# Norm statistics spread by transfers, the image kept in DRAM, two frames, three z tiles and a compact recurrence in a two-layer convolution and attention kernel

## The chip, the cores and the metric

The kernel runs on one core of one Trainium2 chip. The metric is the device time of the whole program in microseconds (us); before the change the median of three runs is 5973.05 us (5971.22 to 5975.53).

## The reference

The input is 32 images of 128 channels and 64 x 64 pixels, all in float32. Layer 0 adds to each image a 3 x 3 convolution of its group-normalized self, with a kernel mixed for each image from four. Layer 1 treats an image as 4096 tokens of 128 channels. It normalizes each token over the channels (norm 1), adds a gated windowed attention (windows of 144, step 72, 4 heads of 4, on 16 channels), normalizes the sum again (norm 2) and adds that to the layer's input; this sum is called x2 here. Then x2 is normalized (norm 3), multiplied by a matrix, batch-normalized over all tokens of all images, and run through a recurrence over the 4096 tokens; its states are added to x2.

```
x = x + conv(gn(x), dyn_k)                       # layer 0
t = to_tokens(x)                                 # 32 x 4096 tokens of 128
n = ln_t(t)                                      # norm 1
out = n + sigmoid(gate) * up(attention(down(n)))
t = t + (out - mean(out)) / sqrt(var(out) + 1e-5) * ln_gamma + ln_beta   # norm 2; this t is x2
Wx = einsum('bti,hi->bth', ln_t(t), W)           # norm 3
Wx = (Wx - mean) * rsqrt(var + 1e-5) * gamma + beta      # over all tokens
step: yt = sigmoid(wx_t + yt @ V.T)
x = from_tokens(t + ys)
```

## The kernel before

Channels lie on the 128 partitions and tokens along the free dimension. Two stages follow each other.

The first stage, `images` (line 331), goes over the 32 images. For each image there are seven jobs, written as Python generators: `load` (fetch, group statistics, mixing of the kernel), `conv`, `project` (norm 1, down projection, queries, keys, values), `attend` (28 steps: scores into the four-bank PSUM tile `sc`, an exponential on ACT, a weighted sum with the exponential as the moving operand), `divide` twice (softmax denominators, up projection into the image's `zt`), and `tail` (norm 2, x2 and its store to the output, norm 3, the product by W, the store of z to DRAM for the second stage). The jobs yield before each step and name the engine, the PSUM tile and the operands that the step needs. A planner in the program that builds the kernel (class `Clock`, line 41, and the loop at line 1074) keeps for each engine the time at which it would be free and takes, among the open jobs, the step that could start first; its prices are in `cost` (line 116). For SP, the engine that issues transfers, it counts 0.8 us of SP for each transfer and a landing time that depends on its size and on the length of its rows. It has no shared DMA bandwidth. The priority of the jobs is the image's number plus an offset for each job (line 1073); `conv` comes last and fills. So the order on each engine is written out when the program is built and doesn't change when something is late: each engine runs its own list in order, and SP does too.

A frame `xs` is a padded image of 66 x 66; there are three, and image b stays in its frame from the fetch until `tail` has added it to make x2. A `zt` tile (4096 tokens) holds an image from norm 1 to the store of z; there are two. The frames' rows are 64 elements, so a fetch moves 256 B pieces; zt is stored in rows of 8 KB.

Norm 1 subtracts the mean by a product with a centring matrix `cen` (8 products of 512 columns, evicted by DVE into zt; `centre`, line 580). `deviations` (line 526) works on half an image: ACT squares, PE sums over the channels with the matrix `avg`, whose result holds different tokens on a few partitions, and `inv_dev` makes the inverse square root from a logarithm, an exponential and four DVE steps. `spread` (line 564) brings these rows back to all 128 partitions by 8 products with `row` into the `sc` tile; DVE multiplies zt by it. This happens for norm 1, norm 2 and norm 3, twice an image each. All operations of this stage are recorded by the planner's helper, so the profile gives line 168 for all of them; they are told apart by their tiles.

The second stage, `by_runs` (line 1541), cuts the 4096 tokens of an image into 128 runs of 32 and starts each run 20 steps early, so that 128 runs advance side by side. A group is two images, 256 columns. Four streams take four groups each; a step is a product with V (PE, into a PSUM tile), a scaled addition of z (DVE, into `h`) and a sigmoid (ACT). In the 20 warming steps the state is in `yw`, which is compact; in the 32 real steps the state is written into the z tile at `zt[:, :, :, r]`, where neighbouring columns lie 32 elements apart, and the next product reads it there (lines 1584 to 1593). Stream j starts 13 j rounds after the first (line 1605). At a group's end GpSimd issues two accumulating transfers that add its states to the output, and SP loads the group six further on into the z tile that comes free (six tiles).

Of the kernel before, what the change touches and what calls it, by code (L numbers as in the profile page):

```python
# [13 lines left out]
P = 128  # L14
EPS = 1e-5
H = W = 64
T = H * W
# [23 lines left out]
class Clock:  # L41
# [22 lines left out]
    @staticmethod  # L64
    def span(ap):

        dims = [(int(s), int(n)) for s, n in ap.ap]
        lo = int(ap.offset) % max(dims[0][0], 1)
        return lo, lo + sum(s * (n - 1) for s, n in dims[1:]) + 1
# [8 lines left out]
    def spot(self, ap):  # L78

        t = ap.tensor  # L80
        if type(t).__name__ != "Tile":
            return None
# [9 lines left out]
    def after(self, eng, ap, write):  # L92
        at = 0.0
        p = self.spot(ap)
        if p is None:
            return at
        lo, hi = self.span(ap)
        psum = "PSUM" in p[0][1].upper()
        for l, h, end, e, w in self.seen.get(p, ()):
            if e != eng and (write or w or psum) and (psum or (l < hi and lo < h)):  # L100
                at = max(at, end + self.LAG)
        return at
# [81 lines left out]
def hybrid_kernel(  # L184
# [34 lines left out]
    k_d = dram.tile([NK, P, 4, 3, P], F32, name="k_d")  # L219
    z_d = dram.tile([NB, P, T], F32, name="z_d")  # L220
# [109 lines left out]

    def images(nc):
# [6 lines left out]
        with ExitStack() as pa:  # L338

            frm = pa.enter_context(tc.tile_pool(name="frm", bufs=1))  # L340
            xs = [frm.tile([P, H + 2, W + 2], F32, name=f"xs{i}") for i in range(3)]
# [4 lines left out]
            def fetch(b):  # L346
                for i in range(4):
                    nc.sync.dma_start(rows(xs[b % 3], 16 * i, 16), x[b, :, 16 * i : 16 * i + 16, :])

            for b in range(3):  # L350
                fetch(b)
# [17 lines left out]
            big = pa.enter_context(tc.tile_pool(name="big", bufs=2))  # L369
# [93 lines left out]
            for q in range(4):  # L463
# [20 lines left out]
            row = kept([P, 2, P], "row")  # L484
            r4 = kept([P, 2], "r4")
            nc.vector.tensor_reduce(
                r4,
                ident.rearrange("p (q r) -> p r q", q=4)[:, 0:2],
                axis=AX.X,
                op=ALU.add,  # L490
            )
            nc.vector.tensor_copy(
                row, r4.rearrange("p (r o) -> p r o", o=1).to_broadcast([P, 2, P])
            )

# [30 lines left out]
            def deviations(src, h, name, mean=False):  # L526

                parts = src[:, part(h)].rearrange("p (c r t) -> p r c t", r=2, t=UNIT)
                for r in range(2):
                    yield "ACT", None, (src[:, part(h)],)  # L530
                    sq = two.tile([P, 4, UNIT], F32, name="sq")
                    nc.scalar.activation(sq, parts[:, r], AF.Square)
# [3 lines left out]
                    if mean and r == 0:  # L536
                        for i in range(2):
                            for c in range(4):
# [5 lines left out]
                                    stop=(i == 1),  # L544
                                )
                    for c in range(4):
# [5 lines left out]
                            stop=(r == 1),  # L552
                        )
                rs = two.tile([P, UNIT], F32, name=name)
                var = ps[:, 0:UNIT]
                if mean:
                    nc.scalar.activation(rs, ps[:, UNIT : 2 * UNIT], AF.Square)
                    nc.vector.tensor_max(sq[:, 1], var, rs)
                    var = sq[:, 1]
                    nc.vector.tensor_sub(var, var, rs)  # L560
                inv_dev(rs, var, sq[:, 0])
                return rs

            def spread(rs):
                ps = sc_tile()
                for r in range(2):
                    for c in range(4):
                        nc.tensor.matmul(
                            ps[:, c, UNIT * r : UNIT * (r + 1)],
                            row[32 * c : 32 * c + 32, r],  # L570
                            rs[32 * c : 32 * c + 32],
                            start=True,
                            stop=True,
                        )
                return ps.rearrange("p c t -> p (c t)")
# [4 lines left out]
            def centre(src, dst, h):  # L580

                for i in range(4 * h, 4 * h + 4):
                    s = slice(i * BLK, (i + 1) * BLK)
                    xi = rows(src, 8 * i)
                    yield "PE", "nm", (xi,)
                    ps = nm_tile()
                    nc.tensor.matmul(ps, cen, xi, start=True, stop=True)
                    nc.vector.tensor_copy(dst[:, s], ps)

            def load(b):  # L590

                while (
                    (b and ("load", b - 1) not in done)
                    or (b > 1 and ("conv", b - 2) not in done)
                    or (b > 2 and ("x2", b - 3) not in done)
                ):
                    yield
                gx = xs[b % 3]
                ks4 = []

                def kernel(k):
                    ks4.append(two.tile([P, 12, P], F32, name="kx"))
                    nc.sync.dma_start(ks4[k], k_d[k].rearrange("p j i l -> p (j i) l"))

                if b > 2:
# [47 lines left out]
                yield "DVE", None, (co, ks4[0])  # L653
                wb = two.tile([P, 12, P], F32, name="wb")
                nc.vector.tensor_scalar_mul(wb, ks4[0], co[:, 0:1])
                for k in range(1, NK):
                    if k + 1 < NK:
                        yield "SP", "kx", ()
                        kernel(k + 1)
                    yield "DVE", None, (co, ks4[k])  # L660
                    nc.vector.scalar_tensor_tensor(
                        wb, ks4[k], co[:, k : k + 1], wb, ALU.mult, ALU.add
                    )
                done["load", b] = wb, gm2

            def conv(b):
# [10 lines left out]
                gx = xs[b % 3]  # L677
# [43 lines left out]
            def project(b):  # L721

                while (
                    ("conv", b) not in done
                    or (b and ("proj", b - 1) not in done)
                    or (b > 1 and ("tail", b - 2) not in done)
                ):
                    yield
                xt = done["conv", b]
                zt = big.tile([P, T + 8], F32, name="zt")  # L730
                nc.gpsimd.memset(zt[:, T:], 0.0)
                rs = []
                for h in range(2):
                    yield from centre(xt, zt, h)
                    rs.append((yield from deviations(zt, h, "rs")))
                for h in range(2):
                    yield "PE", "sc", (rs[h],)
                    ps = spread(rs[h])
                    nc.vector.tensor_mul(zt[:, part(h)], zt[:, part(h)], ps)
# [23 lines left out]
                while b and ("sets", b - 1) not in done:  # L763
                    yield
# [7 lines left out]
                gf = gt.rearrange("p c m d -> p (c m d)")[:, 0:GT]  # L772
                yield "PE", "sc", (gt,)
# [3 lines left out]
                for i, wt in enumerate((wqB, wkB)):  # L777
                    for c in range(2):
# [17 lines left out]
                gtt = xb.rearrange("p u t -> p (u t)")[:, 0 : NWG * P].rearrange("p (m g k) -> p m g k", m=NWG, g=8)  # L796
                nc.gpsimd.tensor_copy(
                    gtt,
                    gf.rearrange("p (m r d) -> p m r d", r=9, d=DK)[:, :, 8:9].to_broadcast(
                        [P, NWG, 8, DK]  # L800
                    ),
                )
# [34 lines left out]

            def attend(b):

                while ("proj", b) not in done or (b and ("div", b - 1, 1) not in done):  # L840
# [883 lines left out]
```

## Time and profile before

| What | Value |
|---|---|
| median of three runs | 5973.05 us |
| the profiled execution | 5971.81 us |
| its span, first to last instruction | 5969.7 us |
| mean granted TensorE clock | 0.945 |
| last step of the images' stage (statistics of z) | 5251.0 us |
| first load of z for the recurrence | 5255.5 us |
| last accumulating store issued | 5944.7 us |

The page gives for each engine its busy time, the span in 40 slices, the transfers, and the costliest groups of instructions with their count, total and mean duration. A slice is 149 us, so the first 35 are the images and the rest the recurrence. HBM traffic is 237.46 MB read and 204.47 MB written. PE's busy time is modelled at the ends of matmuls, so a PE that is busy needn't be at its peak. An fp32 product of N columns appears as two instructions.

### The profile page before, as it was taken

The numbers are of one execution on the slowest core, as the hardware profiler recorded it, in microseconds if no ns is written. First come the engines' busy times: TensorE is split into PE (matmuls) and PEld (weight loads), VectorE is DVE, ScalarE is ACT, GpSimd is POOL, SyncE is SP. The second block draws the span as 40 slices with busy tenths as digits, with TensorE's granted clock in tenths as the row PEclk, the third lists the DMA queues.
The fourth block names the chain that finished last, engine by engine and source line by source line (L and its number), as shares of the span: only waits on it lengthen the run. The fifth ranks groups of instructions, "written<-read, shape, count | busy, mean of one in ns | idle before, by whom it ended". The sixth has DMA issues, their size and how long they took to land. (4 is left out here: it accounts for less than half of the span.)

```text
span 5969.7 us, 107020 instructions
## 1 busy us (share of the span) xinstructions
PE 5209.3 (87%) x46003; PEld 2542.0 (43%) x46003; DVE 3654.7 (61%) x5181; ACT 2558.7 (43%) x3756; POOL 1270.2 (21%) x1049
## 2 busy tenths in 40 slices
PE   2989999999999999999999999899989997669996
PEld 1444444444444444444444444444444443325552
DVE  4555666666666666666666656666566654348884
ACT  0343344433434434444444444344333343348884
POOL 1221222222222222222222222222222221000000
PEclk9999999999999999999999999999999998769996
DMA  5022122221112222222222222122221120046886
GB/s 123 23 66 66 55 66 60 59 66 53 59 55 60 65 66 66 66 66 66 66 66 66 66 66 66 57 64 59 59 58 55 53 60 31 31 198 177 232 204 120
DMA packets 338005, 457.22 MB, mean 77 GB/s; under 512 B 282976, under 2 KB 291440, under 8 KB 308848
## 3 DMA queue, kind: packets, MB, share of 16 engines
q1 hardware_dynamic: 328816, 383.12, 20.5%
q0 software_dynamic: 8704, 67.11, 5.6%
q8 instruction: 368, 6.03, 0.4%
q14 instruction: 117, 0.96, 0.1%
HBM read 237.46 MB, written 204.47 MB: 74 GB/s over the span
## 5 line engine op out<-in xcount | busy, mean ns | idle before, releaser
L168 ACT ACTIVATE ex<-sc 128x1152 f32<-128x1152 f32 x896 | 1013.2, 1131 | 1711.8 <-PE sc L168 1702.3
L168 PE MATMUL nm<-ut,wb 128*128 128x512 f32 x3072 | 1542.5, 630 | 12.3 <-DVE wb L168 12.3
L168 PE MATMUL sc<-qe,ks 32*128 32x288 f32 x7168 | 738.8, 483 | 333.1 <-ACT ext L168 104.6
L168 POOL TENSOR_TENSOR qe<-qs,mqk 128x576 f32<-128x576 f32 x448 | 603.5, 1353 | 1733.2 <-PE sc L168 1729.4
L168 DVE TENSOR_TENSOR xs<-xs,nm 128x512 f32<-128x512 f32 (+1 forms) x640 | 498.0, 795 | 562.8 <-PE nm L168 556.0
L168 PEld LDWEIGHTS nm<-ut,wb 128*128 128x128 f32 x3072 | 543.6, 194 | 683.0 <-issue 659.9
L168 POOL TENSOR_TENSOR ut<-xs 128x576 f32<-128x576 f32 x384 | 524.7, 1397 | 1218.3 <-issue 662.4
L168 PEld LDWEIGHTS sc<-qe,ks 32*128 32x128 f32 x7168 | 303.4, 195 | 862.2 <-issue 289.2
L168 PE MATMUL av<-ex,VE 128*32 128x144 f32 x14336 | 666.1, 307 | 3.9 <-DVE av L168 3.0
L168 ACT ACTIVATE sq<-zt 128x1024 f32<-128x1024 f32 x384 | 402.0, 1056 | 395.4 <-DVE zt L168 392.8
L168 PEld LDWEIGHTS av<-ex,VE 128*32 128x32 f32 x14336 | 377.4, 114 | 348.5 <-issue 277.6
L1587 PE MATMUL v<-zr,fVT 128*128 128x256 f32 x992 | 479.8, 622 | 39.3 <-ACT zr L1592 39.3
L168 DVE TENSOR_TENSOR zt<-zt,sc 128x2048 f32<-128x2048 f32 (+4 forms) x352 | 453.8, 1297 | 49.2 <-PE sc L168 35.1
L1592 ACT ACTIVATE zr<-h,shf 128x256 f32<-128x256 f32 x512 | 372.2, 732 | 129.9 <-DVE h L1588 84.5
L1588 DVE SCALAR_TENSOR_TENSOR h<-zr,scl,v 128x256 f32<-128x256 f32 x512 | 332.0, 651 | 137.4 <-PE v L1587 132.2
L168 PE MATMUL nm<-xs,cen 128*128 128x512 f32 x512 | 270.1, 639 | 48.4 <-DVE zt L168 48.2
L1587 PEld LDWEIGHTS v<-zr,fVT 128*128 128x128 f32 x992 | 176.5, 204 | 238.9 <-ACT zr L1592 206.5
L168 DVE TENSOR_TENSOR sq<-rs 128x256 f32<-128x256 f32 x192 | 81.6, 425 | 302.4 <-ACT rs L168 302.4
L168 DVE SCALAR_TENSOR_TENSOR zt<-sc,gbc,zt 128x576 f32<-128x576 f32 (+1 forms) x192 | 176.0, 917 | 133.4 <-PE sc L168 131.8
L168 PE MATMUL sc<-rs,row 32*128 32x256 f32 x3072 | 221.7, 403 | 34.7 <-ACT ext L168 27.5
L168 PE MATMUL nm<-zt,fWc 128*128 128x512 f32 x512 | 248.3, 617 | 1.4 <-DVE sq L168 1.3
L168 PE MATMUL nm<-sq,avg 128*32 128x256 f32 x3072 | 240.8, 394 | 8.9 <-ACT sq L168 8.9
(191 smaller groups left out, 5697.5 us busy)
## 6 DMA issues: line engine op xcount, KB each, us to landing
kx<-k_d SPq DMA_DIRECT2D x128, 768.0 KB
xs<-in_x_dram SPq DMA_DIRECT2D x128, 512.0 KB
out_dram<-zt SPq DMA_DIRECT2D x64, 1024.0 KB
z_d<-zt SPq DMA_DIRECT2D x64, 1024.0 KB
zr<-z_d SPq DMA_DIRECT2D x32, 2048.0 KB
out_dram<-zr POOLq DMA_DIRECT2D x32, 2048.0 KB, 18.3
k_d<-g SPq DMA_DIRECT2D x4, 768.0 KB
g<-in_conv_k_dram SPq DMA_DIRECT2D x4, 576.0 KB
```

The lines of the kernel that those rows point to most:

```text
L168: got = f(*args, **kw)
L1587: nc.tensor.matmul(ps, fVT, prev, start=True, stop=True)
L1588: nc.vector.scalar_tensor_tensor(h, zt[:, :, :, r], scl, ps, ALU.mult, ALU.add)
L1592: nc.scalar.activation(prev, h, AF.Sigmoid, bias=shf)
```

## The change

- Two scratch tensors in DRAM are new: `r_d` (inverse deviations, and for norm 1 also the mean times the inverse deviation) and `x_d` (the image after the convolution). The planner now tracks `r_d` as one region.
- `deviations` works on a whole image with four blocks of 1024 columns. Its results are stored to `r_d` by four small transfers. `spread` no longer uses PE: it loads quarters of 1024 tokens from `r_d` to all 128 partitions by a broadcasting transfer, into one of five tiles `place`, at most three ahead, and DVE applies them from there. The matrices `row` and the `spread` products are gone.
- Norm 1's mean is summed by PE beside the squares, and subtracted by DVE from a transfer like the deviations; `centre` and its 8 products are gone.
- The image is stored to `x_d` after the convolution, from the frame, in four transfers, and read back by quarters for x2. So a frame is free after norm 1: two frames in place of three, and three zt tiles in place of two.
- An attention may start when the first division of the one before is done, and waits for the second at its tenth set. `av` and `ext` are single tiles. The planner's offsets change.
- The mixed kernel is loaded in halves (8 transfers of 384 KB in place of 4 of 768 KB).
- In the recurrence the state alternates between two compact tiles, GpSimd copies it into the z tile, DVE writes its sum over the product in PSUM, and a stream starts 8 rounds after the one before.

```diff
+    r_d = dram.tile([NB, 3, 2, T], F32, name="r_d")
+    x_d = dram.tile([NB, P, T], F32, name="x_d")
...
+    QT, NPL, NF, NZ = T // 4, 5, 2, 3
...
-            big = pa.enter_context(tc.tile_pool(name="big", bufs=2))
+            big = pa.enter_context(tc.tile_pool(name="big", bufs=NZ))
...
+            places = [kept([P, 4, UNIT], f"place{i}") for i in range(NPL)]
+            spare = list(places)
+
+            def spread(jobs):
+
+                todo, got = list(jobs), []
+                while todo or got:
+                    if todo and len(got) < 3 and spare:
+                        yield "SP", None, (todo[0][0],), (spare[0],)
+                        if spare:
+                            w = spare.pop(0).rearrange("p r t -> p (r t)")
+                            nc.sync.dma_start(w, todo[0][0])
+                            got.append((w, *todo.pop(0)))
+                    elif got:
+                        w, _, aps, use = got[0]
+                        yield "DVE", None, (w,) + aps
+                        use(w)
+                        got.pop(0)
+                        spare.append(w.rearrange("p (r t) -> p r t", r=4))
+                    else:
+                        yield
...
+            def deviations(src, b, k, mean):
...
+                for r in range(4):
+                    sq = yield from place("ACT", (src,))
...
-                        for i in range(2):
+                        for i in range(4):
...
+                if k == 0:
+                    nc.vector.tensor_mul(rs[:, 2], rs[:, 2], rs[:, 3])
+                    n = 2
+                yield "SP", None, (rs,)
+                for c in range(4):
+                    nc.sync.dma_start(
+                        r_d[b, k, n - 2 : 2, QT * c : QT * (c + 1)].rearrange("k (r t) -> r k t", r=4),
+                        rs[32 * c : 32 * c + 4, n:4],
+                    )
...
-                    or (b > 2 and ("x2", b - 3) not in done)
+                    or (b >= NF and ("frame", b - NF) not in done)
...
+                for i in range(4):
+                    nc.sync.dma_start(lines(x_d[b, :, quarter(i)]), rows(xt, 16 * i, 16))
+                yield from deviations(rows(xt, 0, H), b, 0, True)
...
-                for h in range(2):
-                    yield from centre(xt, zt, h)
-                    rs.append((yield from deviations(zt, h, "rs")))
-                for h in range(2):
-                    yield "PE", "sc", (rs[h],)
-                    ps = spread(rs[h])
-                    nc.vector.tensor_mul(zt[:, part(h)], zt[:, part(h)], ps)
+                def normed(i, k):
+                    z = zt[:, quarter(i)]
+                    src = r_d[b, 0, 1 - k, quarter(i)].partition_broadcast(P)
+                    if k == 0:
+                        xi = rows(xt, 16 * i, 16)
+                        return src, (xi,), lambda w: nc.vector.tensor_mul(lines(z), xi, lines(w))
+                    return src, (z,), lambda w: nc.vector.tensor_sub(z, z, w)
+
+                yield from spread(normed(i, k) for i in range(4) for k in range(2))
+                done["frame", b] = True
...
-                while ("proj", b) not in done or (b and ("div", b - 1, 1) not in done):
+                while ("proj", b) not in done or (b and ("div", b - 1, 0) not in done):
...
+                    while b and s == 10 and ("div", b - 1, 1) not in done:
+                        yield
...
+                yield from deviations(zt[:, 0:T], b, 1, False)
+                yield from spread(second(i, k) for i in range(4) for k in range(2))
...
+                yield from deviations(zt[:, 0:T], b, 2, True)
...
+                    yield from spread(third(i) for i in (2 * h, 2 * h + 1))
...
-                    jobs.append([stage == 6, b + (0.7, 0, 0, 0, -0.9, -2.2, 0)[stage], b, g, None])
+                    jobs.append([stage == 6, b + (0.4, -0.3, -0.3, 0.45, -0.65, -2.2, 0)[stage], b, g, None])
...
                     for r in range(RUN):
-                        h = hp.tile([P, NI, NRUN], F32, name=f"h{j}")
                         ps = p_v.tile([P, NI, NRUN], F32, name=f"v{j}")
-                        nc.tensor.matmul(ps, fVT, prev, start=True, stop=True)
+                        nc.tensor.matmul(ps, fVT, yw[1 - r % 2], start=True, stop=True)
                         nc.vector.scalar_tensor_tensor(
-                            h, zt[:, :, :, r], scl, ps, ALU.mult, ALU.add
-                        )
-                        prev = zt[:, :, :, r]
-                        nc.scalar.activation(prev, h, AF.Sigmoid, bias=shf)
+                            ps, zt[:, :, :, r], scl, ps, ALU.mult, ALU.add
+                        )
+                        nc.scalar.activation(yw[r % 2], ps, AF.Sigmoid, bias=shf)
+                        nc.gpsimd.tensor_copy(zt[:, :, :, r], yw[r % 2])
                         yield
...
-            lag = (RUN + WARM) // NSTR
+            lag = 8
```

## The prediction

> **What bounds the kernel now.** I read the page first (busy shares, slices), then the middle of the image stage by windows and waits, then the groups by shape, then the recurrence by windows and timeline. Busy time and the slices:
>
> ```profile
> PE 5209.3 (87%) x46003; PEld 2542.0 (43%) x46003; DVE 3654.7 (61%) x5181; ACT 2558.7 (43%) x3756; POOL 1270.2 (21%) x1049
> ...
> PEclk9999999999999999999999999999999998769996
> ```
>
> There are two stages: images up to about 5255 us, with the granted clock near full, and the recurrence from 5255 to 5970; the dip at the 34th to 36th digit is the images' end and the first streams. Windows of the images' middle (length, then busy us of PE, PEld, DVE, ACT, POOL, then granted clock, DMA share, GB/s), and below it the waits of PE there:
>
> ```profile
> 1000.00:5000.00 4000.00, 3620.53 (x35413) 1762.21 (x35415) 2478.42 (x3346) 1635.03 (x2331) 979.48 (x786) 0.96 0.21 63
> ```
> ```profile
> PE sc L168 <- ACT ext L168: 108.1, 104, 1.3
> PE sc L168 <- POOL qe L168: 64.4, 25, 2.8
> PE sc L168 <- ACT ex L168: 53.3, 104, 0.8
> ...
> PE nm L168 <- DVE zt L168: 38.4, 26, 3.5
> ```
>
> The product that fills kt runs once an image; its starts in the trace are 156.5 us apart (205 to 5055 us in 31 steps). So an image has 142 us of PE work and 15 us of PE idle, most of it attention steps waiting for the exponential. PE is the bound; DVE has 97 us of work in 156. The groups that matter:
>
> ```profile
> L168 PE MATMUL nm<-xs,cen 128*128 128x512 f32 x512 | 270.1, 639 | 48.4 <-DVE zt L168 48.2
> L168 PE MATMUL sc<-rs,row 32*128 32x256 f32 x3072 | 221.7, 403 | 34.7 <-ACT ext L168 27.5 <-DVE zt L168 5.5 <-ACT ex L168 0.9
> L168 PE MATMUL nm<-zt,avg 128*32 128x256 f32 x1024 | 79.6, 435 | 2.4 <-DVE zt L168 2.4
> ...
> L1587 PE MATMUL v<-zr,fVT 128*128 128x256 f32 x992 | 479.8, 622 | 39.3 <-ACT zr L1592 39.3
> L1592 ACT ACTIVATE zr<-h,shf 128x256 f32<-128x256 f32 x512 | 372.2, 732 | 129.9 <-DVE h L1588 84.5
> L1588 DVE SCALAR_TENSOR_TENSOR h<-zr,scl,v 128x256 f32<-128x256 f32 x512 | 332.0, 651 | 137.4 <-PE v L1587 132.2
> L1577 PE MATMUL v<-yw,fVT 128*128 128x254 f32 x608 | 184.0, 411 | 44.5 <-ACT yw L1573 24.8 <-ACT yw L1581 19.6
> L1581 ACT ACTIVATE yw<-h,shf 128x254 f32<-128x254 f32 x304 | 154.2, 507 | 38.9 <-DVE h L1578 33.6
> ```
>
> The first two groups go; the third is what the new mean costs. In the recurrence the same matmul takes 411 ns on compact yw and 622 on zr, whose columns lie 128 B apart, and the sigmoid 507 against 732. Windows again, for a store of long rows, for the 256 B fetch, and for the full recurrence; then the timeline of a small transfer near the images' end:
>
> ```profile
> 2571.00:2573.00 2.00, 2.00 (x7) 1.00 (x6) 2.00 (x2) 0.00 (x0) 0.00 (x0) 1.00 0.95 393
> 2581.00:2587.00 6.00, 3.69 (x72) 2.17 (x64) 4.42 (x10) 3.88 (x7) 1.17 (x1) 1.00 1.36 232
> ...
> 5400.00:5500.00 100.00, 99.38 (x285) 51.63 (x284) 86.79 (x143) 87.03 (x146) 7.44 (x6) 1.00 0.85 210
> ```
> ```profile
> 5185.63 2.71 SPq L168 DMA_DIRECT2D cd<-av  x4
> 5190.07 0.83 DVE L168 RECIPROCAL cd<-cd 128x108 f32<-128x108 f32 x1 [4.47 <-DMA cd<-av]
> ```
>
> Long rows move at 393 GB/s and 256 B pieces at 232. In the recurrence PE, then ACT and DVE, are all close to full, and DMA is at 0.85.
>
> **What the Trainium skill says.** "SBUF — State Buffer", section Door 1 (the note on cachelines): SBUF lines are 16 bytes, and each access that crosses into a new one pays. The trace agrees: 622 against 411 ns. "DMA: Bandwidth & Descriptors", Specifications: pieces under 512 B miss line rate; the trace agrees for loads (232 against 393), and no run here shows such a store to DRAM. Same page, Anatomy of one DMA: about 2 us are completion, so a read of what a DMA wrote waits that long; here 1.7 us pass between the last of four small issues (5188.34) and the reader (5190.07). "TensorE: Matmul & The Clock Gate", Part 1: the array runs at half clock when it has been idle. The trace has 0.50 while one or two streams run, and 1.00 with four.
>
> **The change part by part, images.** Prices are for one image of 32.
> Gone from PE: 8 centring products. One is two instructions of 0.427 us start to start (in runs of convolutions at 2518 us, the same shape), so 6.8 us. 6 spreads of 16 instructions, 1.08 us from start to the next start (2517.05 to 2518.13), 6.5 us. Added: 16 products for norm 1's mean; four of that shape take 0.54 us (5123.58 to 5124.12), 2.2 us. That is -11.1. By busy time of the groups it is (270.1 + 221.7 - 79.6)/32 = -12.9, as these hold pipeline overlap and gaps. The instruction order shows the changes between full and 32-wide products fall from 60 to 48 an image. I take -12, or -384 us in all. What PE still waits for stays: attention score groups with no other product between them are 296 before and 305 after, over the program.
> DVE: it loses 8 copies (0.69), 8 passes of 2048 (four 2.29, four 2.35) and half of six inverse deviations (1.59 each), and gets 20 passes of 1024 at 1.2 (the 1220 ns of the two-source 1024 row) and the means' small steps: 35 us out, 32 in. ACT loses about 2 us. Neither was the bound, so I cost both at nothing; the cover is DVE's 59 us of idle time.
> SP: 28 issues an image become 68: 16 broadcast loads, 4 image loads, 4 image stores, 12 small stores and 4 more kernel loads. DMA work: 8.4 + 2.1 MB at 393 GB/s is 27 us, the store of 2.1 MB in 256 B pieces 9 us at the fetch's rate; with 0.21 x 156 = 33 us before it is 69 of some 145 us. It fits as an average. It does not fit everywhere: the fetch holds SP for 10.7 us (four issues from 2576.55), where the planner charges SP 0.8 each, 3.2 us. The image store is a second such burst. Whatever stands behind a burst on SP is some 7.5 us later than the planner's order supposes: broadcast loads, kernel loads, and the av/cd transfers of the division. Behind a late broadcast load stands its multiply on DVE, and behind that the convolution's evictions, for which PE waits once its three nm tiles are full. Two bursts make 15 us of lateness an image; DVE's idle share (38%) and queued attention steps absorb most, and I let a third through: 5 us, so 160 us. Bounds: nothing if the planner's slack covers it, 16 us if the broadcasts are slow as well (rival B).
> Unknown: a broadcast reads the same 4 KB of DRAM 128 times. No transfer of this size does so before. From below it costs as any long row (1.34 us for 512 KB); from above I take half that rate, as the 256 B pieces show what poor shape costs. I take the first.
> Three zt tiles remove DVE's and POOL's waits for z_d (POOL memset 385 us), none of them PE's but the 1.5 us an image of PE for DVE zt, which is in the 12. Two frames: at the start the third image's fetch waits for the first norm, and the order shows 15 score groups in a row with no convolution, against 1 before; I charge 15 us. Half-size kernel loads, the moved gtt copy and the single ext tile I cost at nothing; attention covers them, and if it doesn't it is under 1 us an image.
> Sum for images: -384 + 160 + 15 = -209.
>
> **Recurrence.** Four streams of 208 steps. A group of two images leaves every 36.2 us (its stores start at 5440.07 and, four groups on, at 5584.83). After: PE 52 x 0.43 = 22 us, ACT 52 x 0.53 = 28, DVE still reads the strided zr: 52 x 0.62 = 32 (starts 5496.72 and 5497.34). DMA: accumulating stores take 5.6% of the span for 32 of them, 10.4 us each, loads 2.1 MB at 400 GB/s 5.3: 2 x 15.7 = 31.4 us a group. So DVE and DMA become the bound together. Rounds: lag 8 instead of 13, so 24 + 208 rounds instead of 39 + 208. 184 full ones at 4 x 0.62 = 2.5 us are 460; 24 at the start and 24 at the end at 2.0 to 2.5 (one stream's step was 2.48 at half clock) 56 each; first load and table 14; the last four stores, 84 us of DMA from 56 us before the end, overhang by 30. Total 616, against 714 (5255.5 to 5969.7). Against it: with lag 8 four groups end within 24 rounds, 60 us, and bring 4 x 31.4 = 126 us of transfers, while only two of six zr tiles are spare; streams 2 and 3 then wait about 18 us at each of three turns, 54 in all, unless queues share well. I take 38: -60. Bounds -98 and 0. POOL gets 512 copies; 896 elements took 0.93 us, so some 0.5 each, 16 of 33 us a group; the next writer of a yw is two steps, 5 us, later. The PSUM target of DVE is priced like SBUF (425 ns against 425 to 440 for 256 elements).
>
> **Sum.** -209 - 60 = -269. The profiled execution took 5971.8 us (span 5969.7), the median 5973.05; so 5703, and I say 5705.
>
> **Rivals.**
> A, all transfers hidden: 5972 - 384 + 15 - 98 = 5505. For it: DMA at 0.21. Against: the bursts.
> B, slower: broadcasts from one DRAM row run at half rate. 16 loads x 1.34 = 21 us later an image, of which three quarters pass through the in-order DVE to PE, 16 us x 32 = 512: 5972 - 384 + 512 + 15 - 60 = 6055. It decides once PE is held over 13.4 us an image ((384 + 60 - 15)/32). For it: loads only three deep. Against: nothing measured is that slow in long rows.
> C, the recurrence gains nothing, stores and loads in bursts being the bound: 5972 - 209 = 5765. For it: DMA at 0.85 already.
>
> **How the numbers follow.** Forecast 0.45 (its own range 5610 to 5820), A 0.18, C 0.15, B 0.22. The range is 5490 to 5990: A and C lie inside, B mostly outside. Faster by over 0.2% (what a measurement can tell from no change) 0.77, within 0.01, slower 0.22.
>
> **What would show it.** PE busy per image near 130 us and an image period near 149; waits of DVE zt for DMA place loads of some us each; a place load landing in 3.5 us (right) or over 5 (B); v<-yw near 411 ns and sigmoids near 0.5; store gaps bunched in fours. Wrong: PE idle above 28 us an image, or the granted clock falling with it.

## The result, and the profile after

The changed kernel took 5714.7 us (median of four runs, 5711.3 to 5717.2) against 5972.1 for the kernel before: a ratio of 0.9575, 95% interval 0.9554 to 0.9596. The profiled execution took 5711.3 us, with a span of 5709.5, so 260.2 us less span than before.

The busy shares and the granted clock on the page of the changed kernel:

```profile
PE 4745.7 (83%) x43443; PEld 2330.2 (41%) x43443; DVE 3681.2 (64%) x5175; ACT 2390.4 (42%) x3564; POOL 1594.0 (28%) x1561
...
PEclk9999999999899899999999999999989989869987
```

PE fell by 464 us, more than the span; DVE, which was to lose a little work, has 27 us more. The product that fills kt (on GpSimd, once an image) starts at 221 us for the first image and at 4867 for the last, 149.9 us an image against 156.4; the first load of the recurrence starts at 5070 and the end is 640 us later (714 before). So the 260 us are: -204 in 31 image periods, +15 at the start, +3 between the last kt product and the first load, -74 in the recurrence.

The middle of the image stage by windows, of the kernel before and then of the changed one (length, then busy us of PE, PEld, DVE, ACT, POOL, then clock, DMA share, GB/s), and the waits of the changed one there (us, times, longest):

```profile
1000.00:4500.00 3500.00, 3170.42 (x31012) 1542.85 (x31010) 2184.40 (x2961) 1431.86 (x2045) 858.46 (x689) 0.97 0.22 64
```
```profile
1000.00:4500.00 3500.00, 3044.74 (x30220) 1477.34 (x30216) 2293.82 (x3030) 1437.68 (x1968) 919.47 (x717) 0.94 0.49 149
```
```profile
DVE zt L173 <- DMA place<-r_d: 116.6, 47, 6.3
...
PE sc L173 <- ACT ext L173: 94.3, 70, 4.7
...
PE av L173 <- DVE av L173: 56.5, 22, 7.2
...
PE sc L173 <- DMA av<-cd: 30.3, 8, 8.6
```

There are 23.4 images in this window (22.4 before). So PE works 130.4 us an image and idles 19.5, where it was 141.7 and 14.7. All DVE waits for DMA come to 13.0 us an image (6.7 before). PE now waits 2.4 us an image for DVE at `av`, the attention's weighted sums, and 1.3 for the transfers of the division (av<-cd); before, it waited for neither.

The groups of the changed kernel by shape (the prediction shows the same groups of before: 622, 651 and 732 ns for product, sum and sigmoid on the strided tile):

```profile
L173 DVE TENSOR_TENSOR zt<-zt,place 128x1024 f32<-128x1024 f32 x256 | 340.0, 1328 | 132.8 <-DMA place<-r_d 97.4 <-ACT zt L173 15.8 <-issue 9.3
...
L1626 PE MATMUL v<-yw,fVT 128*128 128x256 f32 x1024 | 320.1, 439 | 22.6 <-ACT yw L1630 22.1
L1627 DVE SCALAR_TENSOR_TENSOR v<-zr,scl,v 128x256 f32<-128x256 f32 x512 | 308.2, 682 | 28.5 <-PE v L1626 27.1
L1631 POOL COPY zr<-yw 128x256 f32<-128x256 f32 x512 | 302.9, 702 | 381.4 <-ACT yw L1630 220.4 <-DVE v L1621 161.0
...
L1630 ACT ACTIVATE yw<-v,shf 128x256 f32<-128x256 f32 x512 | 241.6, 473 | 82.0 <-DVE v L1627 41.2 <-POOL zr L1631 2.8
...
L173 DVE SCALAR_TENSOR_TENSOR zt<-zt,gam,place 128x1024 f32<-128x1024 f32 x128 | 195.7, 1529 | 79.7 <-DMA place<-r_d 79.1
```

The compact state made the product and the sigmoid cheap, as expected. The passes of 1024 take 1.33 to 1.53 us, not 1.2. Last, the chain of waits in the recurrence; its first turn shows what stands between two groups of a stream:

```profile
5186.40 13.55 POOL zr L1631 x24
...
5200.70 22.79 DMA out_dram<-zr
...
5223.98 24.53 DMA zr<-z_d
...
5253.59 24.87 DMA zr<-z_d
```

A group's store takes 23 us, the load into its tile 25, the next load 25 again, and the chain leads through all of them.

### The profile page after: what moved, and what is told of

Its sections match the earlier page's. It is cut to its first block, busy times and chain, and to the rows that moved or that the text cites. A ratio compares the mean times of both kernels' runs of the same rounds, so it can differ in the third digit from the quotient of the medians.

```text
span 5709.5 us, 105290 instructions
## 1 busy us (share of the span) xinstructions
PE 4745.7 (83%) x43443; PEld 2330.2 (41%) x43443; DVE 3681.2 (64%) x5175; ACT 2390.4 (42%) x3564; POOL 1594.0 (28%) x1561
## 5 line engine op out<-in xcount | busy, mean ns | idle before, releaser
L173 DVE TENSOR_TENSOR zt<-zt,place 128x1024 f32<-128x1024 f32 x256 | 340.0, 1328 | 132.8 <-DMA place<-r_d 97.4
L1631 POOL COPY zr<-yw 128x256 f32<-128x256 f32 x512 | 302.9, 702 | 381.4 <-ACT yw L1630 220.4
L173 ACT ACTIVATE place<-zt 128x1024 f32<-128x1024 f32 x256 | 263.1, 1052 | 207.6 <-DVE zt L173 202.0
L1626 PE MATMUL v<-yw,fVT 128*128 128x256 f32 x1024 | 320.1, 439 | 22.6 <-ACT yw L1630 22.1
L173 DVE SCALAR_TENSOR_TENSOR wb<-kx,co,wb 128x768 f32<-128x768 f32 x192 | 254.0, 1323 | 113.9 <-DMA kx<-k_d 111.9
L1627 DVE SCALAR_TENSOR_TENSOR v<-zr,scl,v 128x256 f32<-128x256 f32 x512 | 308.2, 682 | 28.5 <-PE v L1626 27.1
L173 DVE TENSOR_TENSOR place<-place 128x256 f32<-128x256 f32 x416 | 204.4, 492 | 181.3 <-ACT place L173 172.0
L1620 PE MATMUL v<-yw,fVT 128*128 128x254 f32 x608 | 205.5, 448 | 118.1 <-ACT yw L1617 102.7
L173 PE MATMUL nm<-place,avg 128*32 128x256 f32 x3072 | 238.8, 401 | 54.2 <-ACT place L173 54.0
L173 PE MATMUL nm<-zt,fWc 128*128 128x512 f32 x512 | 262.9, 652 | 17.7 <-DVE xs L173 13.1
L1630 ACT ACTIVATE yw<-v,shf 128x256 f32<-128x256 f32 x512 | 241.6, 473 | 82.0 <-DVE v L1627 41.2
```

The costliest lines, as they stand in the source:

```text
L173: got = f(*args, **kw)
L1620: nc.tensor.matmul(ps, fVT, yw[1 - r % 2][:, :, 1:], start=True, stop=True)
L1626: nc.tensor.matmul(ps, fVT, yw[1 - r % 2], start=True, stop=True)
L1627: nc.vector.scalar_tensor_tensor(ps, zt[:, :, :, r], scl, ps, ALU.mult, ALU.add)
L1630: nc.scalar.activation(yw[r % 2], ps, AF.Sigmoid, bias=shf)
L1631: nc.gpsimd.tensor_copy(zt[:, :, :, r], yw[r % 2])
```

## The experiments

Ratios are to the kernel before, measured beside each. Differences in us are between medians of different sessions, in which the kernel before took 5961 to 5972 us. Periods and times per image come from one profiled execution each.

**1. The recurrence alone.** The kernel before with the changed kernel's whole `by_runs`; the new inner step is

```diff
+                        nc.tensor.matmul(ps, fVT, yw[1 - r % 2], start=True, stop=True)
+                        nc.vector.scalar_tensor_tensor(ps, zt[:, :, :, r], scl, ps, ALU.mult, ALU.add)
+                        nc.scalar.activation(yw[r % 2], ps, AF.Sigmoid, bias=shf)
+                        nc.gpsimd.tensor_copy(zt[:, :, :, r], yw[r % 2])
...
-            lag = (RUN + WARM) // NSTR
+            lag = 8
```

> The kernel before with the changed kernel's recurrence (compact double buffer, sums left in PSUM, copies on GpSimd, lag 8) and nothing else. Theory: the two parts of the change add up, and the recurrence's part is what the traces show between the first load of a stream and the end, 714 us before and 639 after: 5972 - 75 = 5897, between 5885 and 5910, with the stores bunched in fours as in the changed kernel. Rival (my rival C): the compact recurrence alone gains nothing and the shorter tail came from how the image stage ends: within 15 us of 5972.

Measured: 5899.7 us, ratio 0.990 (0.9872 to 0.9928). The image period stayed at 156.0 and the recurrence took 642 us, as long as in the changed kernel (640). So its gain doesn't depend on the change in the images, and rival C falls. The change in the images was not run alone.

**2. Even spacing of the streams.**

```diff
-            lag = 8
+            lag = 13
```

> The changed kernel with the streams 13 rounds apart instead of 8; all else as it is. Theory: with lag 8 four groups finish within 24 rounds and their stores and loads queue together, so that three times about 25 us pass in which streams wait for a load (a cycle of four groups takes 141.7 us where 52 rounds of 2.25 us are 117); with even spacing the stores leave every 30 to 33 us and the recurrence falls from 639 to about 595 us, so 5665 to 5680. Rival 1: the transfers bind as a sum (31.4 us of work a group), spacing changes nothing: stores still every 35 us on average, and 15 more rounds cost about 34 us, so 5745. Rival 2: GpSimd's copies (0.565 us each, 29.4 us a group) bind: about 5690 with the stores far behind the sums.

Measured: 5674.8 us, ratio 0.9514 (0.9492 to 0.9536); the recurrence took 600 us. The issues of the accumulating stores, first in the timeline of the changed kernel, then of this one (start, length of the issue):

```profile
5199.80 2.59 POOL L1634 DMA_DIRECT2D out_dram<-zr  x2
5217.85 2.43 POOL L1634 DMA_DIRECT2D out_dram<-zr  x2
5235.73 2.39 POOL L1634 DMA_DIRECT2D out_dram<-zr  x2
5268.85 2.42 POOL L1634 DMA_DIRECT2D out_dram<-zr  x2
5341.51 2.43 POOL L1634 DMA_DIRECT2D out_dram<-zr  x2
```
```profile
5201.58 2.59 POOL L1634 DMA_DIRECT2D out_dram<-zr  x2
5231.25 2.43 POOL L1634 DMA_DIRECT2D out_dram<-zr  x2
5260.85 2.43 POOL L1634 DMA_DIRECT2D out_dram<-zr  x2
5290.47 2.42 POOL L1634 DMA_DIRECT2D out_dram<-zr  x2
```

With lag 8 four groups leave within 69 us and then none for 73; with lag 13 one leaves every 27 to 33. The windows of 5200 to 5600 us, changed kernel first:

```profile
5200.00:5600.00 400.00, 330.00 (x1142) 184.38 (x1141) 325.78 (x593) 274.74 (x582) 225.36 (x369) 0.90 0.87 231
```
```profile
5200.00:5600.00 400.00, 378.87 (x1340) 203.30 (x1339) 382.01 (x695) 324.00 (x684) 283.59 (x464) 0.99 0.97 250
```

DVE goes from 0.81 to 0.96 of the time and DMA from 0.87 to 0.97. So the sum of the transfers was not the bound of the changed kernel, as the first rival had it; their bunching was. Now both are nearly full. The second rival falls too: in both kernels a group's store is issued 1.1 us after the end of its last sum (once, for the last group, 1.5), so GpSimd's copies keep up.

**3. True prices for SP in the planner.**

```diff
-            return 0.8, 2.5 + (1.2e-5 if run >= 512 else 4e-5) * n * int(out.ap[0][1])
+            return (2.2 if run == 64 else 0.5), 2.5 + (1.2e-5 if run >= 512 else 4e-5) * n * int(out.ap[0][1])
```

> The changed kernel with the planner's price of an SP issue set to what the trace shows: 2.2 us for transfers whose rows are 64 elements (frame fetch, image store) and 0.5 for all others, instead of 0.8 for each. Only the order of the work changes. Theory: the 4.5 us an image that PE idles more than before come from transfers standing behind the two bursts on SP without the planner knowing; with true prices it orders around them, and half or more of it goes: 60 to 140 us faster than the changed kernel, 5575 to 5655. Rival: the idle time comes from the length of the chain of an image (places, DVE passes, attention), which no price on SP changes: within 30 us of 5715.

Measured: 5672.3 us, ratio 0.9503 (0.9472 to 0.9534), period 148.8. A gain of 42 us, between the two expectations; PE's idle time fell from 19.5 to 18.1 us an image. The price was wrong, but little of the idle time comes from it.

**4. No image store.**

```diff
-                yield "SP", None, (rows(xt, 0, H),)
-                for i in range(4):
-                    nc.sync.dma_start(lines(x_d[b, :, quarter(i)]), rows(xt, 16 * i, 16))
...
-                        x_d[b, :, quarter(i)],
+                        x[b, :, 16 * i : 16 * i + 16, :].rearrange("p y w -> p (y w)"),
```

> The changed kernel without the image stores (four issues of 256 B rows an image and 2.1 MB), the second norm's read-back taking the same 512 KB blocks from the input instead; part of the computation is changed by this: the residual of x2 is the input and not the convolved image. Theory: one of the two bursts on SP is gone, so about half of the 5 us an image charged to bursts: 80 us faster than the changed kernel, 5600 to 5670. Rival: the bursts cost nothing and the idle time is elsewhere: within 20 us of 5715.

Measured: 5536.3 us, ratio 0.929 (0.9264 to 0.9317), period 143.9: 178 us, twice the expectation. Windows and waits of this kernel:

```profile
1000.00:4500.00 3500.00, 3136.54 (x31682) 1525.05 (x31682) 2443.51 (x3185) 1506.52 (x2066) 979.54 (x756) 0.96 0.46 141
```
```profile
DVE zt L173 <- DMA place<-r_d: 59.4, 32, 3.1
...
PE av L173 <- DVE av L173: 9.6, 17, 1.1
```

PE idles 14.9 us an image, as before the change, and all DVE waits for DMA are 6.9 us an image, also as before. Without the store the added idle time is gone. Of the 4.6 us, 3.3 stood at the division: PE's waits at `av` fall from 2.4 to 0.4 us and those for av<-cd are gone. The edit takes away SP's time for the store, its transfer and the read-back's need to wait for it, all at once. The next kernels ask by what way the store costs the time.

**5. The store on GpSimd's queue**, the same pieces:

```diff
-                yield "SP", None, (rows(xt, 0, H),)
+                yield "POOL", None, (rows(xt, 0, H),)
                 for i in range(4):
-                    nc.sync.dma_start(lines(x_d[b, :, quarter(i)]), rows(xt, 16 * i, 16))
+                    nc.gpsimd.dma_start(lines(x_d[b, :, quarter(i)]), rows(xt, 16 * i, 16))
```

> The changed kernel with the four issues of the image store on GpSimd's queue instead of SP's; the same 256 B pieces move. Leaving the store out gave 178 us (5.6 us an image). Theory 1, SP's queue is held: the four issues take 2.2 us each of SP and delay the broadcasts, kernel blocks and division transfers behind them; without them on SP most of the 178 us comes back: 5540 to 5600. Theory 2, the transfer itself (2.1 MB in 256 B pieces, 9 to 11 us an image in which other transfers share the engines): the place of issue changes nothing: 5690 to 5730. Theory 3, GpSimd's own work pays for issuing the pieces: slower than the changed kernel.

Measured: 5787.3 us, ratio 0.9713 (0.9679 to 0.9748), slower by 73. From its waits:

```profile
POOL x_d L173 <- DVE xs L173: 313.9, 21, 21.4
...
DVE zt L173 <- DMA place<-r_d: 151.7, 50, 9.0
```

GpSimd now stands up to 21 us at the store, waiting for the last convolution block, with its attention and convolution work behind it. SP has no burst for the store, and yet DVE waits 12.8 us an image for DMA. Freeing SP was therefore not enough. It isn't cleared as a cause either, since the 13.6 us an image that GpSimd stands there are a new cost, which can hide a gain.

**6. The store in long rows**, through a copy by ACT:

```diff
+                    pl_ = yield from place("ACT", (rows(xt, 16 * i, 16),))
+                    pw = pl_.rearrange("p r t -> p (r t)")
+                    nc.scalar.copy(lines(pw), rows(xt, 16 * i, 16))
+                    yield "SP", None, (pw,)
+                    nc.sync.dma_start(x_d[b, :, quarter(i)], pw)
+                    spare.append(pl_)
```

> The changed kernel with each quarter of the image first copied by ACT into a free place (4 x 1.05 us an image) and stored from there in rows of 4 KB, so that SP's issues take about 0.35 us and the transfer 1.3 us a quarter. Theory 1 (SP held by the pieces) and theory 2 (transfer time of the pieces) both give most of the 178 us back, less what ACT and the longer use of the five places cost: 5560 to 5630. Rival: the store costs by its place in the work (it takes places and delays the deviations behind it): 5700 or slower.

Measured: 5715.8 us, ratio 0.9583 (0.9547 to 0.9618), period 150.6: no gain, though the 256 B pieces of the store are gone. The rival's reading fits best, without being shown: the copies need places, and DVE waits 15.2 us an image for DMA. These copies are a new cost too.

**7 and 8. The frame released early.** ACT copies the image into its z tile at once, the frame is free then, and norm 1 works on the z tile; the store leaves from the z tile in 4 KB rows (early_copy) or still from the frame in pieces (early_frame):

```diff
+                for i in range(4):
+                    yield "ACT", None, (rows(xt, 16 * i, 16),), (zt[:, quarter(i)],)
+                    nc.scalar.copy(lines(zt[:, quarter(i)]), rows(xt, 16 * i, 16))
+                done["frame", b] = True
+                yield "SP", None, (zt[:, 0:T],)
+                for i in range(4):
+                    nc.sync.dma_start(x_d[b, :, quarter(i)], zt[:, quarter(i)])
+                yield from deviations(zt[:, 0:T], b, 0, True)
```

> The changed kernel in which ACT copies the convolved image from its frame into its z tile as soon as the convolution is done (4 x 1.05 us), the frame counts as free after these copies instead of after norm 1's spread, the image store leaves from the z tile in rows of 4 KB, and the squares, means and norm 1's passes read the z tile. No SP burst for the store, no 256 B pieces for it. Theory F (two frames hold the image stage: a fetch waits for norm 1 of two images before, and everything between a frame's fetch and its release, 295 us, counts half in the period): the release comes some 100 us earlier, the period falls from 149.9 us to the PE-bound 144 or less: 5540 or faster. Theory D (DVE's in-order chain of spread passes through five places bounds the stage, as one more pass a block arrived whole, 14.4 us an image for some 14 us of DVE): the period stays near 150 and the time within 40 us of 5715.

> As early_copy, but the image store still leaves from the frame in 256 B pieces on SP (its burst and its transfer are as in the changed kernel). Theory F: the early release does it, the burst does not matter much: within 40 us of early_copy. Theory B (the burst and the pieces themselves cost what leaving the store out gave, 178 us): near the changed kernel, 5680 to 5720, with early_copy 130 us or more faster. Theory D: both near 5715.

Measured: 5784.9 us (0.9697, 0.966 to 0.9735) and 5897.2 us (0.9895, 0.9859 to 0.993). Both are slower than the changed kernel, with periods of 152.4 and 155.4 and DVE waiting 20.4 and 18.3 us an image for DMA. Theory F falls. In early_copy's trace the fetch of an image starts 59 us before the kt product of two images earlier (median; 17 in the changed kernel), so the frames are indeed free sooner, and a z tile lies free for 66 us (median) before it is taken again; still the period rises. Between these two, the store in pieces against the store in long rows, lie 112 us, near the 130 of theory B: here the pieces and SP's burst together do cost, though B expected neither kernel to be slower than the changed one.

**9 and 10. More and less DVE work.**

```diff
                         yield "DVE", None, (w,) + aps
+                        nc.vector.tensor_scalar_mul(w, w, 1.0)
                         use(w)
```

> The changed kernel with one more DVE pass for each of the 20 spread blocks of an image: the loaded block times 1.0 onto itself, 1024 elements of one source, about 0.7 us each, 14 us of DVE an image, results unchanged. Theory: DVE has a third of its time idle and its work is hidden, so the passes that cost 1.33 to 1.53 us instead of the 1.2 of the prediction moved nothing: less than 1.5 us an image, 5715 to 5760. Rival: DVE works in order on the path from a broadcast's landing to PE, and a third or more of it arrives at PE: 5 us an image or more, 5870 and above.

```diff
-                    return src, (z,), lambda w: nc.vector.tensor_sub(z, z, w)
+                    return src, (z,), lambda w: nc.vector.tensor_sub(z[:, 0:8], z[:, 0:8], w[:, 0:8])
```

> The changed kernel in which norm 1's subtraction of the spread mean touches 8 columns of each 1024 and not all (that part of the norm is left out): four DVE passes of 1.2 us an image become four of about 0.1, with the same loads and the same waits for them. Theory D (DVE's in-order row of passes sets the image's period; one more pass a block arrived whole): 4 x 1.15 = 4.6 us an image come back whole, 147 us, 5550 to 5590. Rival (only more DVE work hurts, since PE binds again at once below): within 40 us of 5715.

Measured: 6173.0 us (1.0359, 1.0322 to 1.0396), period 164.3, for 20 more passes; and 5687.6 us (0.9524, 0.9502 to 0.9545), period 150.0, for four passes cut short. The window of dve_extra:

```profile
1000.00:4500.00 3500.00, 2844.15 (x27294) 1381.66 (x27291) 2370.19 (x3137) 1305.37 (x1781) 812.66 (x647) 0.89 0.44 134
```

DVE has 13 us more work an image (111.3 against 98.2) and the image takes 14.4 more, with DVE busy in 0.68 of the time; PE's idle time rises to 30.8 us and its granted clock falls to 0.89. Taking 3.8 us of DVE away gains nothing in the period. sub_small is 27 us faster all the same. In the profiled executions it is 22: 12 before the first kt product and 15 between the last one and the first load of the recurrence, less 5 elsewhere. So DVE's idle third is no cover for more work, but DVE time isn't simply the bound either: each of my two theories holds in one direction.

**11 and 12. Both gains together, and true landing times.** The two edits of 2 and 3; then also

```diff
-            return (2.2 if run == 64 else 0.5), 2.5 + (1.2e-5 if run >= 512 else 4e-5) * n * int(out.ap[0][1])
+            return (2.2 if run == 64 else 0.5), 3.8 + (1.2e-5 if run >= 512 else 4e-5) * n * int(out.ap[0][1])
```

> The changed kernel with both edits that gained: streams 13 rounds apart, and SP's issues priced at 2.2 us for rows of 64 elements and 0.5 otherwise. Theory: the two act in different stages and add up: 5715 - 40 - 42 = 5633, between 5615 and 5650. Rival: the end of the image stage and the first loads of the streams overlap differently and one of the two is lost: 5665 or more.

> As prices13, and the planner's time from issue to landing is 1.3 us longer for every transfer (3.8 + size instead of 2.5 + size, so 5.4 us for a 512 KB block, the median that the trace of the changed kernel shows). Theory: DVE waits for DMA 13 us an image because the planner puts its passes ahead of data that land later than it thinks; with the true landing time it puts other DVE work first: 40 to 120 us faster than prices13. Rival: no order helps, since SP waits for DVE and DVE for SP's transfers in a ring of five places: within 25 us of prices13, or slower.

Measured: 5636.8 us (0.9446, 0.9422 to 0.947), the fastest kernel with the full computation here, below the changed kernel by both gains; and 5713.7 us (0.9573, 0.9551 to 0.9595). The waits of the last:

```profile
DVE zt L173 <- DMA place<-r_d: 78.1, 33, 5.8
```

The later landing times did what was expected of DVE: it waits 6.3 us an image for DMA and not 11.9. But the period rose from 148.9 to 151.2. So these waits aren't the cause of the lost time by themselves, and the order chosen by the planner alone is worth 77 us here. Every edit to the image stage also changes that order.

| per image, us | period | PE busy | PE idle | DVE busy | DVE waits for DMA |
|---|---|---|---|---|---|
| before | 156.4 | 141.7 | 14.7 | 97.6 | 6.7 |
| changed | 149.9 | 130.4 | 19.5 | 98.2 | 13.0 |
| no_image_store | 143.9 | 129.0 | 14.9 | 100.5 | 6.9 |
| store_on_pool | 151.9 | 132.3 | 19.6 | 98.3 | 12.8 |
| dve_extra | 164.3 | 133.5 | 30.8 | 111.3 | 9.8 |
| prices13 | 148.9 | 130.7 | 18.2 | 97.5 | 11.9 |
| prices13_land | 151.2 | 130.9 | 20.3 | 98.3 | 6.3 |

The rows are worked out from the windows and waits of 1000 to 4500 us, divided by the number of periods in them.

## Why the prediction was right, and where it was not

**PE's own work: right.** -12 us an image was predicted; PE's busy time fell by 11.3. The granted clock hides a part: it fell from 0.97 to 0.94 in these windows, which the prediction had named, together with more idle time, as a sign of being wrong. In the trace the clock is either 1.0 or 0.5. At 0.5 an instruction of the convolution takes 854 ns from start to start instead of 429, and 13.7 us of an image's PE time lie in such stretches, against 9.9 before. An estimate from these figures is that some 2 us an image of PE's time come from the lower clock. The work then fell by about 13 us, and what was given back is nearer 6.7 us than the 4.8 by which the idle time grew.

**The 5 us an image given back: near in size, not shown in its mechanism.** PE's idle time grew by 4.8 us. The prediction laid this on two bursts on SP, image store and fetch, and let a third of their lateness through; that third was a guess, and that it came out is luck. The fetch's burst was there before, within the 15 us of idle time; the new part goes with the store alone (experiment 4). The step "whatever stands behind a burst on SP is some 7.5 us later" is not shown as its cause: taking the store off SP (5), shortening its issues (6) and telling the planner (3) bring back none, none and 42 of the 178 us. It isn't refuted either. Edits 5 and 6 bring new work with them, each also changes the order, price edits alone moved -42 and +77, and between the two kernels of 7 and 8 the pieces and the burst are worth 112 us. So what carries the cost from the store to PE stays open, and a change of order may hold a part of the 178 us. The frames (7) and DVE's waits for DMA (12) fall as the sole cause. The waits at the division, where most of the idle time went away in experiment 4, do not settle it: in prices13_land they are down to 1.3 us an image, and PE idles 20.3.

**DVE at nothing: wrong in reason, right in outcome.** DVE's sum did not fall by 3 us but rose by 0.6: the passes of 1024 cost 1.33 to 1.53 instead of 1.2, and their small steps 492 ns instead of 425 to 440. The named cover, "DVE's 59 us of idle time", isn't there: 13 us more of DVE made the image 14.4 us longer. The term came out near nothing because DVE's work stayed the same. The terms that the prediction lists as going out add up to 29 us, not 35; the 35 are reached with all six old inverse deviations and their small steps (11.2 us by their groups), and the new ones then stand among the 32.

**Rival A** (all transfers hidden) falls with the 4.8 us of added idle time.

**Broadcasts as long rows: right, but the sign I named for it was bad.** A place load was to land in 3.5 us, or over 5 for rival B. It lands in 5.4 (median from issue, worked out from the 4 KB packets of the trace, 374 loads). Yet a block of 512 KB with distinct rows from `x_d` lands in 4.9; once moving they take 2.15 and 1.95 us, and the shortest 1.39 each. Most of the time to landing passes before the first packet moves (medians 3.2 and 2.9 us), for both. B's mechanism is not there. The image store moves as the fetch does: 13.1 us from first issue to last landing for both, 11.0 for the quickest.

**Start: right in size, but the +15 us at the first kt product isn't the wait that was charged.** Up to that product PE idles less than before (106 us against 113) and runs more of the convolution (192 instructions against 144). The wait stands behind it: the third image's fetch is issued at 193 us instead of 31, and from the first to the second kt product PE idles 23 us instead of 5. Over both stretches PE idles 10 us more.

**Recurrence: right in its mechanism, two sizes off.** It gained 74 us where 60 were predicted. Stores in fours and streams waiting for loads are there; DVE and DMA are the joint bound once the streams are evenly spaced (0.96 and 0.97 of the time in experiment 2). A full round takes 2.25 us and not 2.5 (the sums start 0.56 us apart, not 0.62), which is 184 x 0.25 = 46 us less. The waits at the turns are not 38 but 3 x 24.7 = 74 us: four groups take 141.7 us and 52 rounds only 117. The two errors nearly cancel: 616 - 46 + 74 = 644, against 640. GpSimd's copies were put at 0.5 us and take 0.70 on average. The chain runs through 24 of them before the first store, but they only keep step with the sums: the store is issued 1.1 us after its group's last sum.

**The whole.** The images gained 186 us where 209 were predicted, the recurrence 74 where 60. The two misses have opposite signs, so part of the closeness of the total is luck.

## What to carry to other kernels

When streams share queues for stores and loads, space them so that their turns are even: a shorter stagger saved 15 rounds at the ends and lost more in the middle. A third of idle time on an in-order engine is cover only for work that nobody waits for in turn; test it by adding a known amount before pricing an edit at nothing. Where a planner orders the work from prices, first measure what a change of prices alone does; no effect smaller than that can be put down to the edit that one made.

## What was not expected of the hardware

DVE passes with two sources in SBUF slow down while GpSimd works. From the timelines of DVE and of GpSimd in the changed kernel:

```profile
2235.12 2.17 DVE L173 TENSOR_TENSOR zt<-zt,place 128x1024 f32<-128x1024 f32 x1
```
```profile
2235.02 1.20 POOL L173 TENSOR_TENSOR qe<-qs,mqk 128x576 f32<-128x576 f32 x1 [3.10 <-PE sc L173]
```

GpSimd began 0.1 us earlier and ran for 1.20 us, and the pass took 2.17. Over all 256 such passes, 189 that met no GpSimd instruction took 1.22 us on average, and 23 that lay wholly beside GpSimd's work 1.96. The mixing of kernels on 768 elements goes from 1.01 (84 alone) to 1.79 (51 wholly beside it). The recurrence's sum, which reads one source from PSUM, goes only from 0.66 to 0.69. But a small pass of 256 elements that scales its single source and adds a constant, a step of the inverse deviation, slows down as well:

```profile
4311.14 1.20 DVE L173 TENSOR_SCALAR place<-place 128x256 f32<-128x256 f32 x1
```
```profile
4311.04 1.15 POOL L173 TENSOR_TENSOR qe<-qs,mqk 128x576 f32<-128x576 f32 x1 [3.84 <-PE sc L173]
```

It takes 0.29 us in the 66 cases without GpSimd and 0.75 on average in the 11 wholly beside it. The Trainium skill states this in "SBUF — State Buffer", section Who interferes with whom: a DVE instruction with two SBUF inputs contends with a GpSimd instruction that reads SBUF; one with at most one SBUF input doesn't, unless it runs in one of the 2-port modes, which the section says `tensor_scalar` can enter. The trace agrees for the two-source passes, and for the sum apart from its 5%; whether the small pass runs in such a mode no run here shows. The slowing of the two-source passes is the term that the prediction's 1.2 us left out.
